# Column tiles of 128x64 for every product inside three scan loops

## The chip, the cores and the metric

The kernel runs on one NeuronCore of a Trainium2 chip. The metric is the device time of one execution in microseconds (us). The engines are TensorE (PE, with its weight loads shown apart as PEld), VectorE (DVE), ScalarE (ACT), GpSimd (POOL) and SyncE (SP), which here only issues DMAs. Each has a queue of its own and works it off in order; they wait for each other through semaphores. TensorE multiplies a stationary tile (rows x columns) with a moving one and writes to PSUM.

## The reference

The input x has shape (4, 64, 64, 192): four images of 64 x 64 positions and 192 channels, in float32. Four layers follow, each `x = x + layer(groupnorm(x))`. Three of them are selective scans.

- Layer 0: a projection to 384 channels, a depthwise 3x3 convolution and Silu, then scans along the 4,096 positions in four directions, a norm, a gate and a projection back.
- Layer 1: four mamba blocks on lines of 64 positions (rows and columns, forward and backward). Each projects to 384 inner channels and as many for the gate, convolves 4 taps along the line, scans, gates and projects to 192.
- Layer 2: products with Toeplitz matrices along rows and columns; no scan.
- Layer 3: as layer 0 with 192 inner channels.

The scan is the same in all three, for every inner channel d and 16 states n:

```
x_dbl = x_proj(u)                    # 12 + 16 + 16 values a position: dt, B, C
delta = softplus(dt_proj(dt) + bias) # one value a channel and position
h[d,n] = exp(delta[d]*A[d,n]) * h[d,n] + delta[d]*u[d] * B[n]
y[d]   = sum over n of h[d,n] * C[n]   (+ D[d]*u[d])
```

## The kernel before

A scan is cut into jobs, each one chunk of T = 512 positions in one direction: 32 jobs an image in layers 0 and 3, and 128 jobs for all of layer 1 (four blocks, four images, eight chunks). So each of the three scans has 128 jobs. A job is cut into units: 64 channels by four states, on 128 partitions. Layers 0 and 1 have 384 inner channels (P = 128, NT = 3 groups), that is 24 units a job; layer 3 has 192 (P = 96, NT = 2) and 12 units.

`run_jobs` writes the order out by units. At unit i it emits: `feed` of unit i + 2; `scan` of unit i; `spread` of unit i + 3 where that is a direct unit; `collect` of an earlier pair of units; and then the steps that are due at i, whose places stand in the `when` tables as offsets from the job's own first unit (so that -24 is one job earlier). `plan` gives every load a place. The tile scheduler may still exchange neighbouring instructions on an engine.

The parts of a unit:

- `feed` (L341): PE multiplies dtuT by diagonal matrices of B (`diag`), eight matmuls with a 128x64 stationary tile and 256 moving columns (L361), alternating between the PSUM halves 0:64 and 64:128. The result is b in PSUM. ACT computes dA = exp(A * delta) in two activations (L384). In direct units b comes from POOL (`spread`, L338), and dA goes to the PSUM tile.
- `scan` (L387): DVE scans h from dA and b (L394 over lines in layer 1; L401 with a carry in layers 0 and 3). POOL multiplies by C (L406, hc).
- `collect` (L409): PE folds the two state halves of hc with a 128x64 stationary tile and 512 moving columns and sums in PSUM (L424, y).

Once a job, the steps of `prepare` make delta, B, C and their transposes:

- `project` (L197): x_dbl by chunks. `halves` is true in layer 0 alone: there the 44 columns are padded to 64, and the two halves of a chunk go to PSUM rows 0:64 and 64:128 (L204). Layers 1 and 3 use a [44, 512] tile (L212). ACT copies it to SBUF (xd) and sends B and C to DRAM.
- `turn_b` (L233): PE transposes of B (L238 or L244).
- `step_size` (L247): delta from 12 rows of xd, one matmul of 512 columns (L262), in layer 0 two of 256 with two activations (L254, L259).
- `finish` (L267): softplus and dtu = delta * u.
- `turn` (L276): four PE transposes a group of channels (L279) to the job's tile dtuT, which holds all groups.

Layer 1 adds, in `mamba_job` (L754): the load of xn (48 units ahead of the job's first unit), `input_of` for each of three groups (PE in_ps L779 at -45, -32, -29; a scaled copy and a Silu on ACT; three taps on DVE), `gate` (PE z_ps L779 at -6, -4, -2, Silu on ACT), `gated` (L811), and `out` (two 96-channel halves at +32, +35, PE o_ps L823), which goes to DRAM; backward blocks load the forward result (`earlier`) and add to it. in_ps, z_ps and o_ps are matmuls with 128 or 96 stationary columns over 512 moving ones. ACT loads a table (1.28 us) when it goes from Exp to Silu or Softplus and back.

SP issues all loads in one queue. In layer 1 the tiles both and dtu (L313) are read from DRAM with their 64 rows repeated twice. PSUM holds two tiles each for b, for y and for everything else (mm).

Of the kernel before, what the change touches and what calls it, by code (L numbers as in the profile page):

```python
# [7 lines left out]
F32 = mybir.dt.float32  # L8
# [28 lines left out]
class Kernel:  # L37
# [108 lines left out]
    def plan(self, jobs, order, pools):  # L146
# [3 lines left out]
        for k, job in enumerate(jobs):  # L150
            job["cbc"], job["bbc"], job["diag"], job["both"], job["dtu2"] = {}, {}, {}, {}, {}
            when = {name: k * len(order) + at for name, at in job["when"].items() if isinstance(at, int)}
# [37 lines left out]
    def prepare(self, job, pools):  # L190
# [4 lines left out]
        halves = job["carry"] is not None and NT == 3  # L195

        def project():  # L197
            u = job["u"]
            if halves:

                ps = mm.tile([128, 256], F32, name="xd_ps", tag="mm")
                for t in range(NT):
                    for h in range(2):
                        nc.tensor.matmul(  # L204
                            ps[h * 64 : (h + 1) * 64, :], w["xw"][:, t, :], u[:, t, h * 256 : (h + 1) * 256],
                            start=t == 0, stop=t == NT - 1,
                        )
                xd = job["xd"] = prep.tile([128, 256], F32, name="xd", bufs=1)
            else:
                ps = mm.tile([E, T], F32, name="xd_ps", tag="mm")  # L210
                for t in range(NT):
                    nc.tensor.matmul(ps, w["xw"][:, t, 0:E], u[:, t], start=t == 0, stop=t == NT - 1)  # L212
                xd = job["xd"] = prep.tile([E, T], F32, name="xd", bufs=1)
            nc.scalar.copy(xd, ps)
            job["bc"] = self.bcd.tile([2 * N, T], F32, name="bc_dram")
            if job["carry"] is None:

                by_half = job["bc"].rearrange("(a n) l -> a (n l)", n=2).rearrange(
                    "a (h n l) -> h a n l", h=2, n=2
                )  # L220
                for h in range(2):
                    nc.scalar.dma_start(by_half[h], xd[0 : 2 * N, h * 256 : (h + 1) * 256])
            elif halves:
                by_half = job["bc"].rearrange("a (h l) -> h a l", h=2)
                for h in range(2):
                    nc.scalar.dma_start(by_half[h], xd[h * 64 : h * 64 + 2 * N, :])
            else:
                nc.scalar.dma_start(job["bc"], xd[0 : 2 * N, :])
            job["delta"] = prep.tile([P, NT, T], F32, name="delta", bufs=1)
            job["dtu"] = prep.tile([P, NT, T], F32, name="dtu", bufs=1)  # L230
            job["dtuT"] = prep.tile([128, NB, DI], F32, name="dtuT",)

        def turn_b():  # L233
            bt = job["bt"] = prep.tile([128, NB, N], F32, name="bt")
            if halves:
                ps = mm.tile([128, 2, 128], F32, name="b_ps", tag="mm")
                for k in range(2):
                    nc.tensor.transpose(ps[:, k, :], job["xd"][:, k * 128 : (k + 1) * 128], self.ident)  # L238
                of = ps.rearrange("p k (h e) -> p k h e", h=2)[:, :, :, 0:N]
                nc.scalar.copy(bt.rearrange("p (h k) n -> p k h n", h=2), of)  # L240
                return
            ps = mm.tile([128, NB, N], F32, name="b_ps", tag="mm")
            for k in range(NB):
                nc.tensor.transpose(ps[:, k, :], job["xd"][0:N, k * 128 : (k + 1) * 128], self.ident[:N, :N])  # L244
            nc.scalar.copy(bt, ps)

        def step_size(t):  # L247
            if halves:

                parts = []  # L250
                for h in range(2):
                    parts.append(mm.tile([P, 256], F32, name="dt_ps", tag="mm"))
                    rows = slice(h * 64 + 2 * N, h * 64 + E)
                    nc.tensor.matmul(  # L254
                        parts[h], w["dtw"][rows, t * P : (t + 1) * P], job["xd"][rows, :], start=True, stop=True
                    )
                for h in range(2):
                    to = job["delta"][:, t, h * 256 : (h + 1) * 256]
                    nc.scalar.activation(to, parts[h], AF.Identity, bias=w["dtb"][:, t : t + 1])  # L259
                return  # L260
            dp = mm.tile([P, T], F32, name="dt_ps", tag="mm")
            nc.tensor.matmul(  # L262
                dp, w["dtw"][2 * N : E, t * P : (t + 1) * P], job["xd"][2 * N : E, :], start=True, stop=True
            )
            nc.scalar.activation(job["delta"][:, t, :], dp, AF.Identity, bias=w["dtb"][:, t : t + 1])
# [10 lines left out]
        def turn(t):  # L276
            ps = mm.tile([128, NB, P], F32, name="dtu_ps", tag="mm")
            for k in range(NB):
                nc.tensor.transpose(  # L279
                    ps[:, k, :], job["dtu"][:, t, k * 128 : (k + 1) * 128], self.ident[:P, :P]  # L280
                )
            nc.scalar.copy(job["dtuT"][:, :, t * P : (t + 1) * P], ps)
# [58 lines left out]
    def feed(self, job, t, p, c, pools):  # L341
# [10 lines left out]
        for k in range(0 if direct else NB):  # L352
            for q in range(2):
# [5 lines left out]
                else:  # L359
                    to = half[:, k * 256 : (k + 1) * 256].rearrange("p (l n) -> p n l", n=2)  # L360
                nc.tensor.matmul(  # L361
                    to, job["dtuT"][:, k, g * 64 : (g + 1) * 64], job["diag"][p][:, k, 2 * q : 2 * q + 2, :],
# [170 lines left out]
    def ss2d_scan(self, pre, u_d, y_d, P, NT, ways, A, dtb):  # L533
# [3 lines left out]
        with (  # L537
# [27 lines left out]
            for k, (col, rev) in sorted(enumerate(ways), key=lambda one: one[1]):  # L565
                w = {"dtb": dtb[:, k, :], "A": A[:, k]}

                def weights(k=k, w=w):

                    w["xw"] = pw.tile([P, NT, 64], F32, name="xw")  # L570
                    nc.gpsimd.memset(w["xw"][:, :, E:64], 0.0)
# [583 lines left out]
```

## Time and profile before

| what | value |
|---|---|
| median of 3 runs | 31456.95 us (31430.63 to 31464.33) |
| span of the profiled execution | 31468.7 us, 12 us above that median |
| PE, PEld | 89%, 44% busy |
| DVE, ACT, POOL | 71%, 74%, 73% busy |
| mean granted TensorE clock | 0.947 |
| starts of xd, layer 0 (128 jobs) | 166 to 10229 us, a job mostly 70 to 72 us |
| starts of xd, layer 1 (128 jobs) | 10747 to 21936 us, a job 85 to 90 us |
| starts of xd, layer 3 (128 jobs) | 25230 to 31218 us, a job mostly 39.5 to 40.8 us |
| PE b L361, whole kernel | 12654.8 us busy in 98,304 records |
| PE y L424, whole kernel | 8869.4 us busy in 30,720 records |

The profile is of one execution. The profile's own span is the only time of that execution that is given, so the table sets it beside the median of the three runs. A line of the groups or of the timeline names the source line, the engine, the operation, the tile written and those read, the stationary tile as rows*columns, and the shapes. A PE record's end is modelled, so durations of PE work are better read from the differences of starts. PEclk in the 40 slices is the granted TensorE clock in tenths; the trace also has it as a list of stretches at 1.0 or 0.5.

### The profile page before, as it was taken

The numbers are of one execution on the slowest core, as the hardware profiler recorded it, in microseconds if no ns is written. First come the engines' busy times: TensorE is split into PE (matmuls) and PEld (weight loads), VectorE is DVE, ScalarE is ACT, GpSimd is POOL, SyncE is SP. The second block draws the span as 40 slices with busy tenths as digits, with TensorE's granted clock in tenths as the row PEclk, the third lists the DMA queues.
The fourth block names the chain that finished last, engine by engine and source line by source line (L and its number), as shares of the span: only waits on it lengthen the run. The fifth ranks groups of instructions, "written<-read, shape, count | busy, mean of one in ns | idle before, by whom it ended". The sixth has DMA issues, their size and how long they took to land.

```text
span 31468.7 us, 452840 instructions
## 1 busy us (share of the span) xinstructions
PE 28029.8 (89%) x164120; PEld 13789.1 (44%) x164120; DVE 22494.5 (71%) x16587; ACT 23238.7 (74%) x50564; POOL 22928.7 (73%) x9863
## 2 busy tenths in 40 slices
PE   8998998998899699999999999999588988888888
PEld 4554554554455344444444444444355343434444
DVE  7887887888788677777777777777433277777767
ACT  7885885887688488888888888888133187878787
POOL 7885885887688388888888888888000086877777
PEclk9999999999999899999999999999789999999999
DMA  3333334334333433333332223333533444444444
GB/s 106 101 99 114 102 98 117 99 98 112 102 102 99 135 95 93 95 97 98 97 100 94 93 93 96 98 99 98 133 72 72 109 133 122 129 127 127 124 127 124
DMA packets 1586996, 3327.52 MB, mean 106 GB/s; under 512 B 354981, under 2 KB 374166, under 8 KB 1569142
## 3 DMA queue, kind: packets, MB, share of 16 engines
q1 hardware_dynamic: 1418870, 3021.63, 35.0%
q10 hardware_dynamic: 165888, 276.91, 2.6%
q8 instruction: 1299, 21.28, 0.3%
q14 instruction: 939, 7.69, 0.1%
HBM read 2138.38 MB, written 656.08 MB: 89 GB/s over the span
## 4 chain that ended last, share of the span: by engine, by line
PE 28%; POOL 14%; DMA 10%; DVE 9%; ACT 7%; issue 5%; SPq 2%; DVEq 0%; POOLq 0%; ACTq 0%
POOL hc L406 11%; PE b L361 10%; PE y L424 5%; DVE h L401 4%; DVE h L394 3%; DMA xn<-m_col 3%; DMA xn<-m_row 2%; PE in_ps L779 2%; POOL bs L338 2%; ACT diag L319 2%; SPq L326 2%; ACT dA L384 2%; PE yt_ps L1016 2%; DMA xn<-t_xn 2%; PE dt_ps L262 1%
## 5 line engine op out<-in xcount | busy, mean ns | idle before, releaser
L406 POOL TENSOR_TENSOR hc<-h,c 128x1024 f32<-128x1024 f32 x7680 | 18184.9, 2385 | 3108.4 <-DVE h L394 1267.7
L361 PE MATMUL b<-diag,dtuT 128*64 128x256 f32 x98304 | 12654.8, 391 | 948.3 <-DVE h L401 824.8
L361 PEld LDWEIGHTS b<-diag,dtuT 128*64 128x64 f32 x98304 | 7454.9, 140 | 6818.6 <-issue 3023.4
L401 DVE TENSOR_TENSOR_SCAN h<-dA,carry,b 128x512 f32<-128x512 f32 x6720 | 8187.5, 1264 | 1709.0 <-PE b L361 888.8
L424 PE MATMUL y<-hc,fold 128*64 128x512 f32 x30720 | 8869.4, 602 | 585.3 <-POOL hc L406 571.0
L384 ACT ACTIVATE dA<-both,A 128x512 f32<-128x512 f32 (+1 forms) x12288 | 8311.5, 712 | 310.6 <-DVE h L394 191.2
L394 DVE TENSOR_TENSOR_SCAN h<-dA,b 128x1024 f32<-128x1024 f32 x2304 | 5251.9, 2284 | 2072.9 <-PE b L361 893.8
L319 ACT ACTIVATE diag<-ident,bt 128x128 f32<-128x128 f32 x20480 | 6519.2, 391 | 126.5 <-ACT b L384 83.0
L424 PEld LDWEIGHTS y<-hc,fold 128*64 128x64 f32 x30720 | 2467.3, 138 | 2988.5 <-POOL hc L406 1274.4
L338 POOL TENSOR_TENSOR bs<-dtu,bc 128x1024 f32<-128x1024 f32 x1536 | 3639.2, 2369 | 171.6 <-DMA dtu<-dtu 109.0
L478 POOL MEMSET pad<- 128x13068 f32 (+1 forms) x8 | 73.5, 9188 | 3976.9 <-DMA cb<-in_L_conv_b 3001.7
L384 ACT ACTIVATE b<-both,A 128x504 f32<-128x504 f32 (+1 forms) x3072 | 2078.2, 677 | 273.6 <-DVE h L401 231.0
L394 DVE TENSOR_TENSOR_SCAN h<-b,bs 128x1024 f32<-128x1024 f32 x768 | 1754.3, 2284 | 657.4 <-ACT b L384 388.3
L404 ACT COPY carry<-h 128x2 f32<-128x2 f32 x4608 | 851.8, 185 | 1204.3 <-DVE h L401 985.0
L401 DVE TENSOR_TENSOR_SCAN h<-b,carry,bs 128x512 f32<-128x512 f32 x1344 | 1638.5, 1260 | 105.9 <-POOL hc L406 94.5
L401 DVE TENSOR_TENSOR_SCAN h<-dA,b 128x512 f32<-128x512 f32 x960 | 1113.7, 1205 | 408.2 <-PE b L361 189.0
L384 ACT ACT_TABLE_LOAD x1021 | 1309.9, 1283 | 22.4 <-DMA both<-delta_dram 5.4
L779 PE MATMUL in_ps<-xn,in_w 96*128 96x512 f32 x1536 | 943.2, 745 | 313.5 <-DMA xn<-m_row 159.0
L796 DVE SCALAR_TENSOR_TENSOR u<-in_ps,conv_w,u 128x504 f32<-128x504 f32 (+2 forms) x1152 | 835.9, 726 | 465.1 <-ACT u L791 443.1
L270 DVE TENSOR_TENSOR dtu<-delta,u 128x1536 f32<-128x1536 f32 (+1 forms) x256 | 601.6, 2350 | 529.6 <-ACT delta L269 529.4
L279 PEld LDWEIGHTS dtu_ps<-ident,dtu 128*128 128x128 f32 (+1 forms) x4096 | 422.1, 142 | 881.1 <-issue 556.3
L779 PE MATMUL z_ps<-xn,in_w 96*128 96x512 f32 x1536 | 764.6, 620 | 5.4 <-ACT z L804 5.2
(163 smaller groups left out, 21951.7 us busy)
## 6 DMA issues: line engine op xcount, KB each, us to landing
c<-bc_dram SPq DMA_DIRECT2D x3072, 256.0 KB
both<-delta SPq DMA_DIRECT2D x2048, 128.0 KB
bc<-bc_dram SPq DMA_DIRECT2D x768, 256.0 KB
both<-delta_dram SPq DMA_DIRECT2D x768, 256.0 KB
dtu<-dtu_dram SPq DMA_DIRECT2D x768, 256.0 KB
dtu<-dtu SPq DMA_DIRECT2D x1280, 128.0 KB
L_y<-out ACTq DMA_DIRECT2D x512, 256.0 KB
u<-L_u SPq DMA_DIRECT2D x160, 768.0 KB
```

The lines of the kernel that those rows point to most:

```text
L319: nc.scalar.activation(to, self.ident, AF.Copy, scale=of)
L326: nc.sync.dma_start(one[q * 64 : (q + 1) * 64, :], src.unsqueeze(0).broadcast_to([64, 2 * T]))
L338: self.nc.gpsimd.tensor_mul(by(b), dtu, by(job["bbc"][p]))
L361: nc.tensor.matmul(to, job["dtuT"][:, k, g * 64 : (g + 1) * 64], job["diag"][p][:, k, 2 * q : 2 * q + 2, :], start=True, stop=True,)
L384: nc.scalar.activation(to[n], of, AF.Exp, scale=w["A"][:, g, 2 * p + n : 2 * p + n + 1])
L394: nc.vector.tensor_tensor_scan(h[:, way], dA[:, way], b[:, way], 0.0, ALU.mult, ALU.add)
L401: nc.vector.tensor_tensor_scan(hn[:, n, way], dA[:, n, way], by_n[:, n, way], start, ALU.mult, ALU.add)
L404: nc.scalar.copy(carry[g, p], hn[:, :, 0 if rev else T - 1])
L406: nc.gpsimd.tensor_mul(hc, h, job["cbc"][p])
L424: nc.tensor.matmul(y[c * 64 : (c + 1) * 64, :], self.fold, of, start=first == 0 and n == 0, stop=last == LAST and n == 1)
L779: nc.tensor.matmul(ps, w["in_w"][:, k, to + t * P : to + (t + 1) * P], job["xn"][:, k, :], start=k == 0, stop=k == KC - 1,)
L796: nc.vector.scalar_tensor_tensor(u[:, :, to], ps[:, :, of], tap(3 - j), u[:, :, to], ALU.mult, ALU.add)
```

## The change

All products inside the three scans get a stationary tile of 128 (or 96) rows by 64 columns and write to one half of PSUM's partitions, in pairs, as b and y do already:

- `project` handles both halves of a chunk in every layer, as layer 0 did; x_w comes padded to 64 columns from the host.
- The PE transposes become ordinary matmuls with the identity as the moving tile, two for each 128 positions (`turned`).
- `step_size` multiplies all 128 rows of xd with a stationary tile whose other rows are zero (dt_w is laid out so on the host, 128 x 2 x channels), four matmuls of 256 columns, to one PSUM tile, with one activation of 512.
- dtuT becomes one tile for each group of channels in layers 0 and 1 (four of them in rotation) instead of one for all (two in rotation).
- In layer 1 in_ps and z_ps are written by halves of 64 channels, and the output is cut into 128 channels over 512 positions, and 64 channels over two times 256 positions. Its DRAM tiles become [192, L], and the second part is stored and loaded with two DMAs.

The tiles that ACT, DVE and POOL work on are otherwise the same. The core of the diff:

```diff
 def project():
-            if halves:
+            ps = mm.tile([128, 256], F32, name="xd_ps", tag="mm")
+            for t in range(NT):
+                for h in range(2):
+                    nc.tensor.matmul(
+                        ps[h * 64 : (h + 1) * 64, :], w["xw"][:, t, :], u[:, t, h * 256 : (h + 1) * 256],
+                        start=t == 0, stop=t == NT - 1,
+                    )
...
-                ps = mm.tile([E, T], F32, name="xd_ps", tag="mm")
-                for t in range(NT):
-                    nc.tensor.matmul(ps, w["xw"][:, t, 0:E], u[:, t], start=t == 0, stop=t == NT - 1)
...
+            for h in range(2):
+                nc.scalar.dma_start(by_half[h], xd[h * 64 : h * 64 + 2 * N, :])
...
+        def turned(to, of, p):
+            for half in range(2):
+                nc.tensor.matmul(
+                    to[half * 64 : (half + 1) * 64], of[:, half * 64 : (half + 1) * 64], self.ident[:p, :p],
+                    start=True, stop=True,
+                )
...
 def step_size(t):
-            dp = mm.tile([P, T], F32, name="dt_ps", tag="mm")
-            nc.tensor.matmul(
-                dp, w["dtw"][2 * N : E, t * P : (t + 1) * P], job["xd"][2 * N : E, :], start=True, stop=True
-            )
+            dp = mm.tile([128, T], F32, name="dt_ps", tag="mm")
+            for h in range(2):
+                for half in range(2):
+                    first = t * P + half * 64
+                    nc.tensor.matmul(
+                        dp[half * 64 : (half + 1) * 64, h * 256 : (h + 1) * 256],
+                        w["dtw"][:, h, first : first + 64], job["xd"], start=True, stop=True,
+                    )
...
 def turn(t):
-                nc.tensor.transpose(
-                    ps[:, k, :], job["dtu"][:, t, k * 128 : (k + 1) * 128], self.ident[:P, :P]
-                )
-            nc.scalar.copy(job["dtuT"][:, :, t * P : (t + 1) * P], ps)
+                turned(ps[:, k, :], job["dtu"][:, t, k * 128 : (k + 1) * 128], P)
+            if P == 128:
+                to = job["dtuT"][t] = prep.tile([128, NB, P], F32, name="dtuT", bufs=NT + 1)
...
 def project(t, to, name):          # layer 1: in_ps, z_ps
-                nc.tensor.matmul(
-                    ps, w["in_w"][:, k, to + t * P : to + (t + 1) * P], job["xn"][:, k, :],
+                for half in range(2):
+                    first = to + t * P + half * 64
+                    nc.tensor.matmul(
+                        ps[half * 64 : (half + 1) * 64, :], w["in_w"][:, k, first : first + 64], job["xn"][:, k, :],
...
 def out(m):
-            ps = mm.tile([PC, T], F32, name="o_ps", tag="mm")
+            ps = mm.tile([128, T >> m], F32, name="o_ps", tag="mm")
             for t in range(NT):
-                nc.tensor.matmul(
-                    ps, w["out_w"][:, t, m * PC : (m + 1) * PC], job["z"][:, t, :],
+                for half in range(2):
+                    first, cols = (half * 64, slice(0, T)) if m == 0 else (128, slice(half * 256, (half + 1) * 256))
+                    nc.tensor.matmul(
+                        ps[half * 64 : (half + 1) * 64, :], w["out_w"][:, t, first : first + 64],
+                        job["z"][:, t, cols], start=t == 0, stop=t == NT - 1,
+                    )
...
-            nc.sync.dma_start(done[:, m, s], o)
+            for rows, ch, at in parts(m):
+                nc.sync.dma_start(done[ch, at], o[rows, :])
```

## The prediction

> **What bounds the kernel now.** I read the page first, its busy shares and its 40 slices, then the same by stretches, because the three scans have different limits.
>
> ```profile
> PE 28029.8 (89%) x164120; PEld 13789.1 (44%) x164120; DVE 22494.5 (71%) x16587; ACT 23238.7 (74%) x50564; POOL 22928.7 (73%) x9863
> ...
> PE   8998998998899699999999999999588988888888
> ...
> POOL 7885885887688388888888888888000086877777
> PEclk9999999999999899999999999999789999999999
> ```
>
> ```profile
> 700.00:2200.00 1500.00, 1386.69 (x9906) 763.02 (x9904) 1299.53 (x1071) 1277.28 (x3191) 1335.21 (x572) 0.96 0.38 101
> 14000.00:21000.00 7000.00, 6627.78 (x35480) 2894.03 (x35478) 5011.93 (x2946) 5712.98 (x10515) 6112.29 (x2698) 0.97 0.31 96
> 27000.00:28000.00 1000.00, 910.06 (x5316) 452.00 (x5315) 775.88 (x646) 928.52 (x2359) 895.13 (x375) 1.00 0.50 132
> ```
>
> The rows are the scans of layers 0, 1 and 3; columns PE, PEld, DVE, ACT, POOL, clock, DMA. PE looks like the bound in layer 1 (95%), is level with POOL and DVE in layer 0, and stands behind ACT in layer 3 (93%). Next, the timeline of PE in layer 1, in one job.
>
> ```profile
> 16097.49 0.66 PE L279 MATMUL dtu_ps<-ident,dtu 128*128 128x128 f32 x4
> 16098.07 1.95 PE L361 MATMUL b<-diag,dtuT 128*64 128x256 f32 x16
> ...
> 16119.77 1.98 PE L779 MATMUL in_ps<-xn,in_w 96*128 96x512 f32 x4 [2.26 <-DMA xn<-m_row]
> 16121.69 1.95 PE L361 MATMUL b<-diag,dtuT 128*64 128x256 f32 x16
> 16123.47 1.03 PE L424 MATMUL y<-hc,fold 128*64 128x512 f32 x4
> 16124.42 1.12 PE L262 MATMUL dt_ps<-xd,dt_w 12*128 12x512 f32 x2
> 16125.47 1.95 PE L361 MATMUL b<-diag,dtuT 128*64 128x256 f32 x16
> 16127.25 1.03 PE L424 MATMUL y<-hc,fold 128*64 128x512 f32 x4
> 16128.11 1.90 PE L361 MATMUL b<-diag,dtuT 128*64 128x256 f32 x16
> 16129.84 1.03 PE L424 MATMUL y<-hc,fold 128*64 128x512 f32 x4
> ...
> 16136.64 2.81 PE L823 MATMUL o_ps<-z,out_w 128*96 128x512 f32 x6
> 16139.39 0.87 PE L361 MATMUL b<-diag,dtuT 128*64 128x256 f32 x6
> ```
>
> A float32 matmul makes two records, a transpose one. Take differences of starts. Among 64-column tiles, y's four records (a pair of 512-wide matmuls) cost 0.86 (16127.25 to 16128.11) and b's sixteen (four pairs, 256 wide) 1.73. Going to a full-width product costs y 0.95 instead of 0.86, and the first b behind it 1.78 instead of 1.73: 0.14 us for each excursion.
>
> The job before shows the second thing, a PE at half speed after its wait for xn: the same 4 and 16 records take 2.43 and 2.91 instead of 1.92 and 1.78.
>
> ```profile
> 16032.37 2.50 PE L779 MATMUL in_ps<-xn,in_w 96*128 96x512 f32 x4 [3.02 <-DMA xn<-m_row]
> 16034.80 3.07 PE L361 MATMUL b<-diag,dtuT 128*64 128x256 f32 x16
> 16037.71 1.03 PE L424 MATMUL y<-hc,fold 128*64 128x512 f32 x4
> ```
>
> The clock records give 0.5 there for 6.83 us, once in most jobs. By the starts of xd, 95 of layer 1's 127 jobs take over 88 us (mean 88.8) and 13 under 86 (mean 85.4), the latter mostly without a half-speed stretch; the mean of all is 88.1. The loss is 3.4, half of 6.83; and 88.75 is 26 times 3.413, the step of the clock records, so that the next job meets the same phase.
>
> Third, the DMA packets (start and length) in layer 1: two or more of the 16 engines are at work during 83.9 of a job's 88.1 us, about two thirds of the time exactly two. The loads of line 313, whose source repeats a block twice, fit that pair. The 31% of the window hides it: a job can't fall far under 84, whatever PE does.
>
> Last, ACT in layer 1, groups and then a wait:
>
> ```profile
> L384 ACT ACT_TABLE_LOAD x475 | 609.4, 1283 | 7.6
> L799 ACT ACT_TABLE_LOAD x238 | 305.4, 1283 | 41.7 <-DVE u L796 38.8
> L804 ACT ACT_TABLE_LOAD x158 | 202.7, 1283 | 1.8
> ```
>
> ```profile
> DVE h L394 <- ACT dA L384: 483.4, 161, 6.1
> ```
>
> Between 16083.6 and 16107.7 ACT works almost without a pause (Silu and Exp tables in turn), the scan waits for its dA and POOL starves 2.6 and 3.4 us.
>
> **The change part by part, per job.** PE in layer 1:
> - in_ps and z, six times: 1.92 and 0.14 before, now two pairs of 512, 1.72: -0.34 each, -2.0.
> - dt, three times: 1.05 and 0.14, now two pairs of 256, 0.86: -0.33 each, -1.0. Both halves now read all 128 rows, as b does.
> - o, twice: 2.75 and 0.14, now three pairs of 512 and three of 256, 3.87 in all: -1.9.
> - xd: six records 0.429 apart, 2.57, now what layer 0's halves take, 1.40: -1.2.
> - turn, three times: 0.58 and 0.14; now four pairs of 128-wide real matmuls. No row has them. By columns a pair is half of b's, 0.22; loads that do not overlap could double it, 0.44. The nearest row, layer 2's 64x64 products, takes 0.110 a pass for a pair though half as wide as these, so 0.22: 0.88 in all, +0.15 each, +0.45 (high end +3.1). turn_b: 0.45 to 0.44.
>
> The sum is -5.6 us a job, or -720 over 128 jobs if PE alone decided. It does not; what lies on the path is this:
> - Behind xn's wait, in_ps and two dt save 1.0, but POOL, next on the path, idles only 0.72 there in the job without a slow clock; the in_ps at 16077 saves 0.34 inside a POOL wait of 0.80. I take -1.1 (ends -0.3, all of it hidden by DMA, and -1.5).
> - xd's 1.2 goes into the wait for h behind it (1.15 now); o's runs beside POOL's unbroken 16052 to 16076; a shorter z only waits for ACT.
> - Against it: the scheduler reorders ACT. In its order for the changed kernel, layer 1 has 1,730 table loads instead of 1,522, in 105 of 127 jobs 14 instead of 12, since u's and z's Silu no longer share one. The two lie in the saturated stretch: 2.57 us. Walking its order with the rows' durations, the direct unit's b comes 3.7 late, and the last dA only 1.0, because copies and diagonals move ahead into pauses. Ends 0 and +2.1 (2.57 in 83% of jobs); I take +0.8.
>
> So a job without the slow clock goes from 85.4 to 85.1 (84 by the DMA pair to 87.2). With it, 88.5: no multiple of 3.413 any more, so the phase drifts and the slow stretch strikes only some jobs. I take 4 in 10 (ends none and all): 85.1 + 0.4 x 3.4 = 86.4, or -1.7 x 128 = -216 us.
>
> The Trainium skill, "TensorE: Matmul & The Clock Gate", section "Why this matters for your kernels", allows PE gaps up to about 3 us. Measured here, 2.1 to 2.8 us before in_ps already halve the clock; by the page those jobs would lose nothing, and layer 1 would end at 85.1, -380 us. The measurement decides, and it speaks against the change: a faster PE waits longer.
>
> Layer 0 (xd is in halves already): dt goes from 0.73, four records of which two run side by side, to 0.86; turn +0.15; together +0.84 a job, +108 at most. ACT takes three 512-wide instead of six 256-wide activations (mean 0.462 each), about -0.6. Half-speed stretches of up to 6.83 us follow a PE wait of 4.1 to 4.7 there, and most jobs last 71.7, 21 steps of the clock; a small delay shortens that stretch instead. Taken +30 (-20 to +108).
>
> Layer 3: xd 1.72 to 0.93, dt twice 1.13 to 0.86, turn twice 0.57 to 0.88: -0.7 a job. ACT, the busier, gets a second DMA issue (0.65) and a shorter copy (0.579 to 0.351): +0.4. Taken -20 (-95 to +54).
>
> No cost taken: SP issues one more DMA at each out and earlier (0.5 each, behind xn and before c loads that wait for POOL anyway); the larger dtw (384 KB) comes once per direction, its memset on POOL is gone; o's copy and add shrink by 256 columns; dtuT's four tiles are free before they are needed.
>
> Sum: -216 + 30 - 20 = -206. The profiled span is 31468.7, 12 above the median of the runs: 31250.
>
> **Rivals.**
> - *Down to the DMA pair.* No slow stretch in layer 1, jobs near 84.3: -3.8 x 128 = -490, total 30970. For it: the 85.4 us jobs exist. Against: xn still arrives when the pair's backlog lets it, and PE waits sooner.
> - *The same lock.* ACT's loads eat what PE gives, the loop stays at 85.3 or above, and 88.75 holds: +0.65 x 128 = +80, total 31550 with the other layers at +10. For it: the sum of -1.1 and +0.8 is near nothing.
> - *Slower by ACT's loads.* If the 3.7 us delay of the direct unit reaches SP's loads in 83% of jobs, a job takes 88.1 + 3.1 - 1.1 = 90.1: +260, total 31710; it decides as soon as more than 1.1 of it passes. Against: xn stands 13 us behind in the queue, so that SP has slack.
> - *PE does not shrink*, should 128-wide tiles cost 0.44 a pair: +2.6 a job more in layers 0 and 1 (twelve pairs), 0.6 of these 680 us on the path: about 31650.
>
> **How the numbers follow.** Forecast (31000 to 31394) 0.43; DMA pair 0.12; same lock 0.27, of it 0.12 within 0.2% (63 us, about what a measurement of this kernel can tell from no change) and 0.15 above; the two slower ones 0.18. Hence faster 0.55, same 0.12, slower 0.33. Leaving out about one in ten on each side, the range is 30980 to 31690; the forecast's own is 31000 to 31394.
>
> **What would show it.** In layer 1: records 128*64 only; y before dt 0.86 apart; PE's share down from 95% to about 91%; 1,700 table loads; xd starts 85 to 87 apart instead of 88.8; the DMA pair at work 84 us a job still. Layer 0 within 0.5 us of 71.1 a job, layer 3 of 40. Wrong if jobs lock at 88.7 or above, if DVE's wait for dA grows from 6.1 us a job (483.4 over 79) past 9, or if turn takes over 1.2 us.

## The result, and the profile after

The changed kernel takes 31642.88 us (median of four runs, 31637.2 to 31650.66) against 31460.64 for the kernel before on the same chip (31430.63 to 31475.7): a ratio of 1.0058, 95% interval 1.0044 to 1.0072. It is slower by 0.58%. The forecast of 206 us less had the wrong sign, although its range held the time.

The profiled execution spans 31641.4 us, 173 more than that of the kernel before. The starts of xd divide the scans. Layer 0's four scans add up to 8598.2 us (8615.8 before, -18), layer 3's to 4826.6 (4850.1 before, -23). Layer 1 goes from 10730.3 to 22125.6, 11395.3 us against 11189.2: +206. So layer 1 alone is to be explained; a job there went from 88.2 to 89.9 us (means without the first three jobs).

First the page after, its shares and four of its 40-slice rows:

```profile
PE 27491.3 (87%) x189464; PEld 16459.4 (52%) x189464; DVE 22376.5 (71%) x16587; ACT 23377.2 (74%) x50388; POOL 22882.0 (72%) x9831
...
PE   8998998998899689888888998888588988888888
...
POOL 7885885886788388888888888888100077777777
PEclk9999999999999899999999999999788999999999
```

Then the stretch of layer 1 that the prediction showed, by engine (columns PE, PEld, DVE, ACT, POOL, clock, DMA share, GB/s):

```profile
14000.00:21000.00 7000.00, 6195.43 (x42505) 3745.05 (x42502) 4842.23 (x2883) 5756.24 (x10436) 5980.31 (x2645) 0.97 0.31 94
```

PE fell from 6628 to 6195 us of the 7000, and in the same time POOL did less: 2645 instructions instead of 2698. PE was freed, and the kernel did not follow it. Next the groups of ACT and one of PE in that stretch:

```profile
L374 ACT ACT_TABLE_LOAD x531 | 681.3, 1283 | 6.8
L786 ACT ACT_TABLE_LOAD x232 | 297.7, 1283 | 21.1 <-DVE u L783 19.0 <-issue 0.2
L791 ACT ACT_TABLE_LOAD x221 | 283.5, 1283 | 3.0
L766 PE MATMUL in_ps<-xn,in_w 96*64 96x512 f32 x1864 | 646.0, 622 | 249.4 <-DMA xn<-m_col 137.6 <-DMA xn<-m_row 111.7
```

The gate's Silu (line 791, before 804) loads a table 221 times in 77 jobs instead of 158 in 79. The last row's idle time is PE's wait for xn: 249.4 us, 3.2 a job, against 191.5 or 2.4 before. Last, the waits (us in total, times, longest):

```profile
POOL hc L396 <- DVE h L384: 942.3, 344, 7.9
DVE h L384 <- PE b L351: 659.0, 241, 10.7
ACT u L778 <- PE in_ps L766: 596.8, 151, 10.7
DVE u L783 <- ACT u L778: 548.6, 164, 6.4
...
DVE h L384 <- POOL hc L396: 380.1, 255, 5.4
DVE h L384 <- ACT dA L374: 326.1, 114, 5.4
```

The wait named in the prediction as a sign, the scan's for dA, fell: 4.2 us a job (326.1 over 77) instead of 6.1. Others grew. DVE's taps of the convolution wait for ACT's scaled copy of in_ps 7.1 us a job (548.6 over 77; 279.2 over 79 or 3.5 before), and ACT waits for in_ps 7.8 (596.8 over 77; 355.2 over 79 or 4.5 before).

**Where a job loses the time.** POOL works 77.1 us a job in both kernels, and a job is that plus POOL's idle time. So I added up POOL's idle time ahead of each of a job's 24 products with C (hc), as a mean over 122 jobs of layer 1, in us:

| kernel | products 1-3 | 4-6 | 7-10 | 22 | all 24 | job |
|---|---|---|---|---|---|---|
| before | 6.8 | 0.1 | 3.4 | 0.8 | 11.0 | 88.2 |
| after | 4.4 | 3.8 | 0.2 | 4.3 | 12.8 | 89.9 |

The change won 2.4 us at the start of a job and 3.2 at products 7 to 10, and lost 3.7 at products 4 to 6 and 3.5 at the 22nd. The gain at 7 to 10 and the loss at 4 to 6 belong together: both are the wait for xn, which strikes earlier in the job after the change, and e5 and e6 below remove the one and the other by the same move. What is left as a cost is the 22nd product. The two losses can be read from the timeline.

*Product 22.* ACT, DVE and POOL in one job of the changed kernel; columns start, duration, engine, line, operation, tiles, count, and in brackets the idle time before and its releaser. The tile b that ACT writes is the dA of a direct unit.

```profile
15609.30 0.72 ACT L786 ACTIVATE u<-u,conv_b 128x512 f32<-128x512 f32 x1
15609.93 0.16 ACT L362 COPY b<-zero 128x16 f32<-128x16 f32 x1
15610.11 1.28 ACT L374 ACT_TABLE_LOAD   x1
15611.40 0.72 ACT L374 ACTIVATE dA<-both,A 128x504 f32<-128x504 f32 x1
15612.14 1.28 ACT L791 ACT_TABLE_LOAD   x1
15613.43 0.60 ACT L791 ACTIVATE z<-z_ps 128x512 f32<-128x512 f32 x1
15614.05 1.28 ACT L374 ACT_TABLE_LOAD   x1
15615.34 0.68 ACT L374 ACTIVATE b<-both,A 128x504 f32<-128x504 f32 x1
15615.96 0.67 ACT L778 ACTIVATE u<-in_ps,conv_w 128x512 f32<-128x512 f32 x1
15616.53 0.67 ACT L374 ACTIVATE b<-both,A 128x504 f32<-128x504 f32 x1
```

```profile
15607.95 2.28 DVE L384 TENSOR_TENSOR_SCAN h<-dA,b 128x1024 f32<-128x1024 f32 x1
15616.66 0.74 DVE L783 SCALAR_TENSOR_TENSOR u<-in_ps,conv_w,u 128x504 f32<-128x504 f32 x1 [6.43 <-ACT u L778]
15617.32 2.28 DVE L384 TENSOR_TENSOR_SCAN h<-b,bs 128x1024 f32<-128x1024 f32 x1
```

```profile
15619.75 2.37 POOL L396 TENSOR_TENSOR hc<-h,c 128x1024 f32<-128x1024 f32 x1 [5.12 <-DMA c<-bc_dram]
```

The same place in the kernel before, ACT and then DVE:

```profile
15561.14 0.72 ACT L799 ACTIVATE u<-u,conv_b 128x512 f32<-128x512 f32 x1
15561.88 1.28 ACT L384 ACT_TABLE_LOAD   x1
15563.17 0.68 ACT L384 ACTIVATE b<-both,A 128x504 f32<-128x504 f32 x1
15563.88 1.28 ACT L804 ACT_TABLE_LOAD   x1
```

```profile
15559.59 2.28 DVE L394 TENSOR_TENSOR_SCAN h<-dA,b 128x1024 f32<-128x1024 f32 x1
15563.96 2.29 DVE L394 TENSOR_TENSOR_SCAN h<-b,bs 128x1024 f32<-128x1024 f32 x1 [2.09 <-ACT b L384]
15566.36 2.29 DVE L394 TENSOR_TENSOR_SCAN h<-dA,b 128x1024 f32<-128x1024 f32 x1
```

Before, ACT ends the second half of the direct unit's dA 2.7 us after it began u's Silu, and only then loads the table for z. After, z's Silu with its two loads stands ahead of both halves. The direct unit's scan starts 8.0 us after the start of u's Silu (15617.32 against 15609.30) instead of 2.8 (15563.96 against 15561.14). DVE is empty for 6.43 us, and POOL behind it for 5.12 in this job. The profile names a load of c as what released POOL, but the product starts 0.15 us after the scan's end here, and 0.14 us in the median job of both kernels: it waits for the scan.

That ACT's order does this, and not the time that the new products take on PE, shows inside the changed kernel. In 102 of the 122 jobs z's Silu stands ahead of both halves, and POOL idles 5.1 us before product 22; in the other 20 it stands behind them, with the same new products, and POOL idles 0.9. From u's Silu to the second half ACT pauses for 0.1 us in all, as a mean over the jobs: it waits for nothing there.

*Products 4 to 6.* PE and then DVE early in a job of the changed kernel:

```profile
15552.33 1.08 PE L766 MATMUL in_ps<-xn,in_w 96*64 96x512 f32 x1 [4.34 <-DMA xn<-m_row]
15552.34 1.12 PE L351 MATMUL b<-diag,dtuT 128*64 128x256 f32 x2
...
15556.60 1.08 PE L766 MATMUL in_ps<-xn,in_w 96*64 96x512 f32 x4
```

```profile
15556.92 2.29 DVE L384 TENSOR_TENSOR_SCAN h<-dA,b 128x1024 f32<-128x1024 f32 x1 [8.38 <-PE b L351]
```

in_ps now consists of four matmuls instead of two, and the order has put the first of them ahead of a unit's eight b matmuls and the other three behind. In the rows b starts at 15552.34, right behind the first in_ps at 15552.33: this b waits for xn too, and the scan with it. A unit's b stands between the pieces of in_ps in 81 of the 96 waits for xn of over 1 us in the changed kernel, and in none of 122 in the kernel before.

### The profile page after: what moved, and what is told of

It is laid out like the page before. It is cut to its first block, busy times and chain, and to the rows that moved or that the text cites. A ratio compares the mean times of both kernels' runs of the same rounds, so it can differ in the third digit from the quotient of the medians.

```text
span 31641.4 us, 503746 instructions
## 1 busy us (share of the span) xinstructions
PE 27491.3 (87%) x189464; PEld 16459.4 (52%) x189464; DVE 22376.5 (71%) x16587; ACT 23377.2 (74%) x50388; POOL 22882.0 (72%) x9831
## 4 chain that ended last, share of the span: by engine, by line
PE 32%; ACT 20%; DVE 15%; POOL 15%; DMA 9%; issue 8%; SPq 1%; ACTq 1%; DVEq 0%; POOLq 0%
PE b L351 12%; POOL hc L396 11%; ACT diag L305 7%; DVE h L391 7%; PE y L414 6%; ACT dA L374 5%; DVE h L384 3%; DMA xn<-m_col 2%; DMA xn<-m_row 2%; POOL bs L324 2%; PE yt_ps L1018 2%; ACT b L374 2%; DMA xn<-t_xn 2%; PE conv_ps L500 2%; POOL dtu L254 1%
## 5 line engine op out<-in xcount | busy, mean ns | idle before, releaser
L351 PE MATMUL b<-diag,dtuT 128*64 128x256 f32 x98304 | 13293.5, 389 | 1212.0 <-DVE h L391 720.5
L351 PEld LDWEIGHTS b<-diag,dtuT 128*64 128x64 f32 x98304 | 8701.4, 139 | 5531.3 <-issue 1840.9
L414 PE MATMUL y<-hc,fold 128*64 128x512 f32 x30720 | 10297.8, 604 | 918.1 <-POOL hc L396 896.8
L414 PEld LDWEIGHTS y<-hc,fold 128*64 128x64 f32 x30720 | 3121.3, 138 | 3147.3 <-POOL hc L396 1904.1
L226 PEld LDWEIGHTS dtu_ps<-ident,dtu 128*64 128x64 f32 (+1 forms) x16384 | 1185.7, 140 | 559.9 <-issue 283.7
L374 ACT ACT_TABLE_LOAD x1125 | 1443.4, 1283 | 18.2 <-DMA both<-delta_dram 4.0
L226 PE MATMUL dtu_ps<-ident,dtu 128*64 128x128 f32 (+1 forms) x16384 | 1374.4, 274 | 64.1 <-DVE dtu L254 41.6
L766 PE MATMUL in_ps<-xn,in_w 96*64 96x512 f32 x3072 | 1052.8, 626 | 390.5 <-DMA xn<-m_row 199.1
```

Of the source, the lines that this page charges most:

```text
L226: nc.tensor.matmul(to[half * 64 : (half + 1) * 64], of[:, half * 64 : (half + 1) * 64], self.ident[:p, :p], start=True, stop=True,)
L351: nc.tensor.matmul(to, dtu, job["diag"][p][:, k, 2 * q : 2 * q + 2, :], start=True, stop=True,)
L374: nc.scalar.activation(to[n], of, AF.Exp, scale=w["A"][:, g, 2 * p + n : 2 * p + n + 1])
L414: nc.tensor.matmul(y[c * 64 : (c + 1) * 64, :], self.fold, of, start=first == 0 and n == 0, stop=last == LAST and n == 1)
L766: nc.tensor.matmul(ps[half * 64 : (half + 1) * 64, :], w["in_w"][:, k, first : first + 64], job["xn"][:, k, :], start=k == 0, stop=k == KC ...
```

## The experiments

Each ratio is to the kernel before on the same chip, where its median lay between 31453 and 31472 us.

**The gate's second product one unit later (e1).** The edit, on the changed kernel:

```diff
-        ... each(gate, (-6, -4, -2)) ...
+        ... each(gate, (-6, -3, -2)) ...
```

> The changed kernel with one number altered: the second product for the gate in layer 1 is placed at -3 instead of -4 units. Written out, its Silu then stands behind that of u in 125 of 127 jobs and shares the table, so that a job has 12 table loads instead of 14. Theory (the additional table loads lengthen the stretch from the last in_ps to the next xd, which took 20.4 us on the mean after the change and 18.2 in the 21 jobs with 11 or 12 loads): that stretch goes to 18.2 in all jobs and a job to between 84.5 (as those 21) and 86.4 (with a slow clock in 4 jobs of 10); total 30970 to 31210. Rival, the new products themselves or the additional DMAs are what costs: the loads go, the job stays near 89.9, total 31640 within 60. Rival, the clock: the loads go, but the half-speed stretch now strikes in most jobs and locks them near 88.7, total 31490.

Measured: 31342.39 us (31337.43 to 31351.7), 0.9958 of the kernel before (0.9945 to 0.9972). The second group of rows below shows the 12 loads:

```profile
L374 ACT ACT_TABLE_LOAD x476 | 610.7, 1283 | 7.3
L786 ACT ACT_TABLE_LOAD x238 | 305.4, 1283 | 3.6 <-issue 0.5
L791 ACT ACT_TABLE_LOAD x158 | 202.7, 1283 | 1.8
```

One placement is worth 300 us, more than the whole change costs. But the theory missed by 130 us, and its mechanism was wrong: the stretch from the last in_ps to the next xd did not go to 18.2 but to 21.9, and POOL still idles 5.0 us before product 22, since the first Silu of z, which this edit leaves at -6, stands ahead of the direct unit's dA in all 122 jobs. The gain is at products 1 to 6, 3.9 + 0.1 instead of 4.4 + 3.8, less 1.3 at products 7 to 10: PE still waits for xn (245.9 us in the same 7000), but all of in_ps stands again behind the b of the unit that it had held up, as in the kernel before. By these idle times the gain came from the order of PE and not from the number of loads.

**Ten loads (e2).** The same line with `(-5, -3, -2)`.

> The changed kernel with the gate's three products at -5, -3 and -2 instead of -6, -4 and -2. Written out, two gate Silus follow u's last one, and a job has 10 table loads. Theory of the loads: at least as good as with 12; the pair of DMA engines that is at work 80 to 82 us in the fastest jobs lets a job fall little below 84, so 83.5 to 85.5, total 30850 to 31100. If the stretch from the last in_ps to the next xd is bound by ACT still, it goes from 18.2 to about 16; if DMA sets the end, the rest of the job grows by what it loses. Rivals as for the other placement: 31640 if the loads do not matter, 31490 if the clock locks.

Measured: 31303.16 us (31292.49 to 31311.96), 0.9947 (0.9931 to 0.9962). The job takes 87.1 us, the idle time before product 22 is 4.5: z's Silu with its loads now stands between the two halves of the direct unit's dA in all 122 jobs. Expected was 83.5 to 85.5: a miss, for the same reason as above. Two more loads gone are worth 39 us.

**Two more loads in the kernel before (e3).**

```diff
             nc.scalar.activation(u, u, AF.Silu, bias=w["conv_b"][:, t : t + 1])
+            if t == 2:
+                nc.scalar.activation(tiny, job["u"][:, t, 0:1], AF.Exp, scale=0.0)
...
-            nc.scalar.activation(job["z"][:, t, :], project(t, DI, "z"), AF.Silu)
+            nc.scalar.activation(job["z"][:, t, :], project(t, DI, "z"), AF.Silu, scale=tiny if t else 1.0)
+            if t == 1:
+                nc.scalar.activation(tiny, job["z"][:, t, 0:1], AF.Exp, scale=0.0)
```

> The kernel before with one more pair of table loads in each job of layer 1 and nothing else of the change: two Exp of 128x1 elements between u's and z's Silu (their result, a one, scales z) separate what shared a table; 14 loads instead of 12 in 125 jobs. Theory of the loads: the stretch from the last in_ps to the next xd goes from 18.0 to between 20.2 and 20.9 us (2.57 of loads, some 0.3 of the two small activations), a job by 2.2 to 2.9, total 31460 + 280 to 360 = 31740 to 31820. Rival, ACT has room there and the increase came from other parts of the change: total within 60 of the kernel before.

Measured: 31764.21 us (31761.1 to 31768.17), 1.0092 (1.0078 to 1.0106), so +293; a job takes 90.6. The total is as expected, the place only in part: the stretch from the last in_ps to the next xd grew by 0.9 us, and POOL's idle time by 1.3 before product 22, 3.1 at products 4 to 6 and 1.3 at products 1 to 3, while 3.4 at products 7 to 10 went. It shows that a pair of loads there costs nearly its 2.6 us (a job is 2.4 longer) and is not hidden; it does not show that the changed kernel loses by them in this way.

**Layer 1 as before (e4).** The methods of layer 1 and its preparation are those of the kernel before, layers 0 and 3 those of the changed one.

```diff
-            for at, step in self.prepare(job, pools) + job["steps"]:
+            for at, step in (self.prepare if job["carry"] is not None else self.prepare_lines)(job, pools) + job["steps"]:
```

> The changed kernel with layer 1 as it was, so that only layers 0 and 3 have the new products. By the two traces layer 0's four scans went from 2154.0, 2156.2, 2153.1 and 2152.5 us to 2150.4, 2152.0, 2145.8 and 2150.0 (-18 in all) and layer 3's from 1212 to 1207 each (-21). If that is the change's doing, the total is 31460 - 39 = 31420, within 20. If it was the accident of one execution, the total is that of the kernel before within 20.

Measured: 31419.08 us (31379.31 to 31469.27, 11 runs) against 31471.62, a ratio of 0.9986 (0.9977 to 0.9994). The other two layers are faster by some 44 us, by the ratio of the runs. Its profiled execution agrees: the scans of layers 0 and 3 add up to 8594.8 and 4826.0 us, 21 and 24 less than before. So layer 1 costs the rest and more.

**The first in_ps four units later (e5, e6, e7).** On the kernel before, on the changed one, and on the changed one with the gate of e2:

```diff
-        steps += [(-48, load)] + each(input_of, (-45, -32, -29)) + ...
+        steps += [(-48, load)] + each(input_of, (-41, -32, -29)) + ...
```

> The kernel before with the first product of the input projection (in_ps of t = 0) placed at -41 instead of -45 units, four units (some 14 us) after the place where PE waited for xn; u's first Silu then also falls beside the Softplus, so that a job has 11 table loads instead of 12. Theory (the wait for xn and the half-speed stretch that follows it cost layer 1 what lies between 88.2 and 85 us a job): in layer 1 the PE gap before in_ps (2.4 us a job) and the clock records of 0.5 (5.6 us a job) go, a job takes 84.0 to 85.3, total 31470 less 125 times 2.9 to 4.2 = 30950 to 31110. Rival, the wait only moves to another place because a pair of DMA engines sets the pace and everything else follows: a job stays above 87 and the total within 100 of the kernel before.

> The same move in the changed kernel; Silus of z and u still stand apart in most jobs, 12 or 13 table loads. Theory of the loads together with the wait: the two are separate, so that the changed kernel gains half of its slow clock (4.3 us a job, 2.1) and most of the gap before in_ps (3.2 us), and keeps the additional loads: a job of 89.9 goes to 85.5 to 87, total 31110 to 31300, slower than the kernel before with the same move by 100 to 250. Rival, the additional loads only cost because they delay xn: then both kernels with this move are within 60 of each other, or the changed one is ahead.

> The changed kernel with both moves: the gate at -5, -3, -2 and the first in_ps at -41; nine table loads a job. Theory: with neither the loads nor the wait for xn, the pair of DMA engines is what is left (84.1 us in the fastest jobs, with at least two engines at work in 80 to 82 of them): 83.5 to 84.5 a job, total 31303 less 125 times 2.6 to 3.6 = 30850 to 30980. Rival: it stays at 87 because another wait takes its place; total 31300.

Measured: 31102.32 us (0.9884, 0.9869 to 0.9899), 31239.68 (0.9927, 0.9913 to 0.9942) and 31016.23 (0.9857, 0.9842 to 0.9871). The jobs take 85.4, 86.9 and 85.1. The row of in_ps in e5 shows that PE no longer waits:

```profile
L779 PE MATMUL in_ps<-xn,in_w 96*128 96x512 f32 x984 | 488.0, 618 | 0.0
```

Records of a half-speed clock fell from 5.6 to 1.6 us a job. The wait for xn and what follows it cost the kernel before 2.8 us a job, 350 us in all; one load less is in that. With that gone from both, the changed kernel is still 137 us behind the kernel before with the same move; layer 1 alone, from first to last xd, takes 11004.1 us against 10823.8, so that 180 of the 206 us remain without the wait. POOL's idle time at products 4 to 6 is 0.2 in e6, at product 22 still 4.1: that is what remains. e7 missed its range by 36 us.

**Ten loads in the kernel before (e8).** Its gate at `(-7, -4, -2)`.

> The kernel before with the gate at -7, -4, -2 instead of -6, -4, -2: z's Silus pair with u's, 10 table loads a job and nothing else of the change. Theory of the loads: one pair less is worth what it was from 12 to 10 loads in the changed kernel (87.6 to 87.1 a job, -0.4) up to what it was from 14 to 12 (-2.3): a job takes 85.9 to 87.8, total 31170 to 31410. Rival, the lock of the half-speed stretch: the job stays at 88.7 and the total within 60 of the kernel before.

Measured: 31505.22 us (31493.85 to 31512.78), 1.0017 (1.0008 to 1.0027). The rival holds: jobs take 88.5, half-speed clock 6.5 us a job. PE's wait before in_ps grew from 2.4 to 3.8 us a job (302.1 over 79): the loads that are taken away give nothing here, because the wait for xn takes it back.

**The turn of dtu undone, in all three layers (e9).**

```diff
-                turned(ps[:, k, :], job["dtu"][:, t, k * 128 : (k + 1) * 128], P)
+                nc.tensor.transpose(
+                    ps[:, k, :], job["dtu"][:, t, k * 128 : (k + 1) * 128], self.ident[:P, :P]
+                )
```

> The changed kernel with one part undone: the turn of dtu by PE transposes again, all other products as changed. Written out, ACT's order for layer 1 then has 10 table loads in 125 jobs instead of 14. Theory (what lengthened layer 1 is ACT's order, which the slower turn brings about: the loads around the first gate Silu hold up the direct unit's dA, and POOL idles 4.3 us before the job's 22nd product against 0.8 in the kernel before): that idle time goes back to 0.8 to 1.5, a job of 89.9 takes 85.5 to 87.5, total 31070 to 31330, ahead of the kernel before. Rival, the other products or the order of PE (in_ps one unit earlier, behind which the next b waits for xn) make the increase: the job stays above 88.5 and the total above 31460.

Measured: 31481.73 us (31472.56 to 31503.16), 1.0005 (0.9996 to 1.0014): the same as the kernel before, 161 us less than the changed one. POOL's idle time before product 22 is 0.9 again, as the theory said; but the job takes 88.8, not 85.5 to 87.5. The rows of in_ps and of the loads:

```profile
L768 PE MATMUL in_ps<-xn,in_w 96*64 96x512 f32 x1888 | 656.3, 752 | 531.3 <-DMA xn<-m_col 340.1 <-DMA xn<-m_row 191.2
...
L793 ACT ACT_TABLE_LOAD x156 | 200.1, 1283 | 2.8
```

PE waits for xn 6.8 us a job (531.3 over 78) instead of 2.4, and the clock records of half speed are 8.1 us a job instead of 5.6. A job is no shorter than before: what the other products save on PE is spent in front of xn. No b stands between the pieces of in_ps any more (124 waits), though in_ps has four matmuls here too.

**The turn alone, in layer 1 of the kernel before (e10).**

```diff
+                for half in range(2):
+                    nc.tensor.matmul(
+                        ps[half * 64 : (half + 1) * 64, k, :], of[:, half * 64 : (half + 1) * 64], self.ident,
+                        start=True, stop=True,
+                    )
```

> The kernel before with this one part of the change alone, in layer 1: the turn of dtu as pairs of real products with 64 columns. Written out, 14 table loads in 125 jobs instead of 12, as in the changed kernel. Theory: the order does it; a job of 88.2 takes what it took with the loads put in by hand (90.6), or up to 1.8 more because turn takes 0.6 us longer on PE three times: 90.0 to 92.4, total 31690 to 31990. Rival, the turn alone does no harm and the increase needs the other products: total within 60 of the kernel before.

Measured: 31664.3 us (31660.76 to 31685.32), 1.0062 (1.0045 to 1.0079): +196 us, about what the whole change costs (+182, and +206 in layer 1 alone), and 26 below the range given. Its waits and its gate's loads:

```profile
POOL hc L412 <- DVE h L400: 878.1, 273, 5.7
DVE u L802 <- ACT u L797: 615.4, 155, 6.4
```

```profile
L810 ACT ACT_TABLE_LOAD x234 | 300.2, 1283 | 3.2
```

The loads of z's Silu (234 in 78 jobs), the longest wait of 6.4 us of the taps and 5.2 us of POOL's idle time before product 22 are all there, with one part of the change. So is the torn in_ps: one of its two matmuls stands ahead of a unit's b and one behind in all of 121 waits for xn, although in_ps itself is as it was. The turn brings both losses, by the order.

**The loads of both and dtu cut in two (e11 on e7, e12 on the changed kernel).**

```diff
-            nc.sync.dma_start(one, src.unsqueeze(0).broadcast_to([2, 64, T]))
+            for q in range(2):
+                nc.sync.dma_start(one[q * 64 : (q + 1) * 64, :], src)
```

> The changed kernel with the gate at -5, -3, -2, the first in_ps at -41, and in layer 1 the loads of both and dtu as two DMAs of 64 rows each instead of one that reads the 64 rows twice. If the pair of DMA engines that these loads use holds the job at 84 us, the job of 85.1 falls towards POOL's 77.4 of work plus the idle time that ACT causes, 80 to 83, total 30380 to 30760. Rival, the pair was never what the job waited for (the loads wait for their buffers on SP's queue, 2056 us of 7000 behind POOL's bs): the job stays at 84.5 to 85.3, total within 60 of 31016.

> The changed kernel with only the loads of both and dtu in layer 1 cut in two. If xn takes 12 us from its issue to in_ps because it stands behind these loads on two of the engines, it now lands sooner: the PE gap before in_ps (3.2 us a job) and POOL's idle time before the job's fifth product (3.3 us a job) go, a job of 89.9 takes 86 to 87.5, total 31150 to 31340. Rival, xn is late for another reason (it is issued late, or all 16 engines are busy): no change, total within 60 of 31640.

Measured: 30961.36 us (30960.43 to 30966.88; 0.9837, 0.9822 to 0.9852) and 31152.38 (31138.71 to 31156.11; 0.9897, 0.9882 to 0.9911). In e12 the job takes 86.2 and the row of in_ps has no wait left:

```profile
L767 PE MATMUL in_ps<-xn,in_w 96*64 96x512 f32 x1944 | 633.0, 594 | 0.0
```

xn lands 4 to 6 us after its issue (median 4.8). In the changed kernel in_ps started some 12 to 14 us after the issue. POOL's idle time at products 4 to 6 went from 3.8 to 0.1; the 4.3 before product 22 stay. With two lines altered in the DMAs the changed kernel becomes 1.03% faster than the kernel before. In e11 at least two DMA engines are at work in 38 us of a job instead of 84, and the job only goes from 85.1 to 84.7, as the rival said: it was not the pair that held it there.

The kernels of these runs in one table, POOL's idle time a job as above (e4 has layer 1 as before):

| kernel | products 1-3 | 4-6 | 7-10 | 22 | all 24 | total us |
|---|---|---|---|---|---|---|
| e1 gate at -3 | 3.9 | 0.1 | 1.5 | 5.0 | 10.5 | 31342 |
| e2 gate at -5, -3, -2 | 3.7 | 0.0 | 1.9 | 4.5 | 10.1 | 31303 |
| e3 before, two loads more | 8.0 | 3.2 | 0.0 | 2.1 | 13.4 | 31764 |
| e5 before, in_ps later | 6.8 | 0.1 | 0.6 | 0.8 | 8.3 | 31102 |
| e6 after, in_ps later | 4.6 | 0.2 | 0.2 | 4.1 | 9.7 | 31240 |
| e7 after, e2 and e6 together | 3.5 | 0.0 | 0.0 | 4.4 | 8.0 | 31016 |
| e8 before, gate at -7 | 4.7 | 0.0 | 5.4 | 0.9 | 11.3 | 31505 |
| e9 after, turn undone | 6.0 | 0.0 | 4.7 | 0.9 | 11.7 | 31482 |
| e10 before, turn alone | 6.0 | 1.4 | 0.1 | 5.2 | 12.7 | 31664 |
| e11 best | 3.2 | 0.0 | 0.0 | 4.4 | 7.6 | 30961 |
| e12 after, loads cut | 4.5 | 0.1 | 0.0 | 4.3 | 9.1 | 31152 |

**What stays open.** The kernel before with the loads cut in two was not run, so it is not known whether the change wins or loses once xn comes early by that means; nor the turn undone together with the cut loads and the later in_ps, which might go below 30961 by the table (0.9 instead of 4.4 before product 22) if no other wait takes it back. That the order, and not the turn's own PE time (0.6 us longer, three times), holds up the direct unit is shown by the 20 jobs of the changed kernel with the old order there; no run keeps the old order in all jobs, so the turn's own PE time has no price of its own. Why the order comes out differently with the new turn was not examined.

## Why the prediction was wrong

**The step that failed: "I take +0.8" for ACT's loads.** The prediction walked ACT's order and found that "the direct unit's b comes 3.7 late, and the last dA only 1.0", and priced the late b at nearly nothing because the last dA was hardly late. But a scan stands on DVE in order: when the direct unit's scan and the taps ahead of it wait, no later scan can pass them. The delay reached POOL almost whole: in place of the 0.8 taken, 3.5 us a job before product 22. The upper end of +2.1 was too low as well, since it priced two loads and not the place at which they stand.

**The second step: the wait for xn.** It was taken to shorten ("behind xn's wait, in_ps and two dt save 1.0"). It grew from 2.4 to 3.2 us, and one in_ps matmul ahead of a unit's b made it a wait of the scan (8.38 us in the job shown): 3.7 us a job at products 4 to 6, where the kernel before had lost 3.4 at products 7 to 10. The prediction did not look at where the four pieces of in_ps stand among b in the order. e6 and e12 remove this loss by two different means. It is the smaller of the two: with the wait gone from both kernels (e5, e6) 180 of layer 1's 206 us remain.

**The drifting clock.** Slow records did become fewer, 5.6 to 4.3 us a job, and the jobs left the lock at 88.75: they spread from 84 to 95. The forecast's 3.4 in 4 of 10 jobs would have been 2.7 us of records; e9 shows what the products without the turn would have brought: 88.8 us a job and more half speed, the rival of the same lock. So the main gain of -216 was wrong for its own reason too: in e9 the quicker PE stands longer in front of xn, 6.8 us a job instead of 2.4.

**PE's own sum.** The products shrank as said. A turn whose 16 records stay together takes 0.87 us at full clock (136 of the turns in e10's stretch), just the 0.88 taken. But most turns of the changed kernel are torn apart among other products, and their records take 3.64 us a job in start-to-start time (1.2 each; 2.90 or 1.0 each in e10) against 1.76 a job (0.59 each) before. By its own mark (over 1.2 us) it was at the edge. PE's share in the stretch is 88.5%, below the 91% named.

**Table loads, layers 0 and 3.** Loads came as said, 14 a job. Layer 0 was taken at +30 and gave -18, layer 3 at -20 and gave -23; e4 confirms their sum (-44, interval -0.23% to -0.06%). Small slips in the reading, on which the sum does not hang: by the starts of xd 99 and not 95 of layer 1's jobs take over 88 us and 17, besides the first, and not 13 under 86, and the first of the two POOL waits in the stretch of ACT is 2.85 us and not 2.6.

**The floor of 84 us.** The pair of DMA engines did not hold the job: e11 ends at 84.7 with the pair relieved. That was read from a count of busy engines without asking which instruction waited for them. But the loads on the pair did make xn late, which e12 shows.

**The rivals.** "Slower by ACT's loads" was nearest: 90.1 a job and 31710 against 89.9 and 31643. It named the late b of the direct unit, but let it act through SP's loads; by the timeline it acts through DVE. So its nearness is partly luck. "PE does not shrink" has the time (31650) without the mechanism: PE did shrink.

## What to carry to other kernels

Where an order is written out for engines that work in order, an edit to one engine's products can also rearrange the others; read the new order for what stands ahead of each scan, and price a late operand by the next thing on its engine's queue that cannot pass it, not by how late the last one is. Before speeding up an engine, look for the wait in front of which it will stand: here one later in_ps and loads in two smaller DMAs took 403 and 490 us off the changed kernel, whose products took none. A product of several matmuls can be torn apart by the order, cut finer or not (e10), so that a piece that waits for a load holds up other work.

## What the runs showed of the hardware

- The load that reads 64 rows twice in one DMA kept at least two DMA engines at work in 85 to 88 us of most jobs of the changed kernel, and xn came 12 to 14 us after its issue. As two DMAs of 64 rows, the time with two or more engines at work fell to 38 us, that with exactly two from 52 to 1, and xn landed within 4 to 6. The Trainium skill, "DMA: Bandwidth & Descriptors", section "Why a DMA increments its semaphore by 16 and not by 1", lets the size of the slowest dimension decide over how many of up to 16 engines a transfer is spread; that size is 2 in the one form, hence two engines, and 64 in the other, hence 16. The counts of engines at work agree; which engines a load used is not in the trace.
- Turning 128x128 values as a pair of real products with 64 columns took 0.22 us where the four pairs of a turn ran in one block (0.87 for four, e10). Over all turns it took 0.24 us in e10 and 0.30 in the changed kernel, where other products stand between (2.90 and 3.64 a job over twelve, start to start), a PE transpose 0.15 (1.76 over twelve).
- A table load took 1.283 us everywhere, but the time did not follow their number: ten loads a job came with 31505 us (e8), 31482 (e9) and 31303 (e2).
- In layer 1 of the kernel before, a wait of PE before in_ps of over 1 us (median 2.4, mostly 1.9 to 3.2) was followed by a half-speed stretch in 106 of 122 jobs. Most of these stretches last 6.83 us, and 90 of 106 start 88.75 us after the one before, 26 times the 3.413 of the clock records. With the wait gone (e5) the half-speed records fell from 5.6 to 1.6 us a job.
